# A two-layer Winograd convolution: fewer row operations in the input transform, two products added by TensorE onto used PSUM banks, 1/std inside VectorE's transform, fixed output buffers

## The chip, the cores and the metric

The kernel runs on one core of a Trainium2 chip. Five engines work side by side, each through its own list of instructions in order: TensorE (PE in the profile, its weight loads as PEld), VectorE (DVE), ScalarE (ACT), GpSimd (POOL), and SyncE (SP), which only issues DMAs here. They wait for each other by semaphores. The metric is the device time of the whole program in microseconds; shorter is better.

## The reference

Two equal layers, each a group normalisation (16 groups of 2 channels, no gain or bias), a 5x5 convolution with reflected edges, 32 to 32 channels, and a residual. The FFT in the reference is only one way to write the convolution.

```
def _gn(v, G=16, eps=1e-5):
    g = v.reshape(B_, G, C_ // G, H_, W_)
    m = jnp.mean(g, axis=(2, 3, 4), keepdims=True)
    s = jnp.var(g, axis=(2, 3, 4), keepdims=True)
    return ((g - m) / jnp.sqrt(s + eps)).reshape(v.shape)
...
xp = jnp.pad(x, ((0, 0), (0, 0), (2, 2), (2, 2)), mode='reflect')
...
# x: (8, 32, 252, 252) float32, weights (32, 32, 5, 5)
x = x + _L0_conv_ref(_gn(x), L0_conv_weight)
x = x + _L1_conv_ref(_gn(x), L1_conv_weight)
```

## The kernel before, in words

**Layout.** An image is split by the parity of its rows and columns into four planes; with 32 channels that makes 128 partitions. One parity row holds 126 values, padded to 128. In this layout the 5x5 filter is a 3x3 one with 128x128 matrices, and along the rows it is done as a Winograd transform F(6,3): 8 input rows become 8 transformed rows `v0`..`v7`, each takes part in one product (3 matmuls, one per column tap `b3`, 128x378, in float32, which the profile shows as two MATMUL records each, so 48 records a step), and the 8 products `m0`..`m7` are combined to 6 output rows.

**Steps.** A step (b, l, T) is 18 parity rows of image b in layer l (3 tiles of 6 rows). An image has 7 steps a layer (T = 0 to 6). The 112 steps stand in 16 phases of 7: (0,0), (1,0), (0,1), (2,0), (1,1), ... (7,0), (6,1), (7,1), written as (image, layer). The instruction order is written out by hand (`manual_schedule`); each engine runs its list in that order. What is written in iteration i of the main loop:

- SP: x of step i+4 (`fetch`, layer 0), two chunks of x for the statistics of a later image (`input_chunk`, three buffers `sx`), and the transformed weights `u` of the next phase at the phase's sixth step.
- DVE: `transform` of step i+1 (`e`, `p`, `q`, then `v1`..`v6`), then the output combination of step i.
- POOL: `differences` of step i+2 (`a` = rows 3-6 minus 1-4, `e` = rows 4-7 plus 0-3, over 4 rows each) and `ends` of step i+1 (`v0`, `v7` as two rows of differences of `e`). The first is held behind the last instruction of `transform` by a dependency of its own.
- PE: `m1`..`m6`, `m0`, `m7` of step i, each in a PSUM bank of its own (8 banks in turn).
- ACT: copies of `m1`, `m3`, `m5` out of PSUM (`a1`, `a3`, `a5`); after `a1` `prepare` of step i+3 (layer 0: four copies x to `g` and the padding columns; layer 1: DMAs from a scratch tensor instead); after `a3` and `a5` the outgoing work of step i-1 (layer 0: padding of y, DMAs to scratch, two passes for sums; layer 1: two pairs of copies into `o`, then DMAs to the output); after `a5` the sums of two chunks of x, in four steps of a phase.

`m1`'s copy adds the bias; DVE forms s1, d1 = a1 +- m2; then m3, m4 and m5, m6 are turned in place into difference and sum ("pairs"), and y takes `2^j` times the first pair and `0.5^j` times the second; at last `m0` is added to row 0 and `m7` to row 5.

**The boundary.** In the last step of a phase (`late`), the normalisation of the next phase is made: DVE takes mean and variance from a PSUM tile, ACT the square root, DVE 1/std with one Newton step (`scales`, six instructions on one value a partition), ACT multiplies the 128x3072 weights by it (`scale_matrices`), DVE adds the identity part for the residual (`add_own`). Before the change `scales` stands behind the whole transform, `scale_matrices` behind `a3`, and `add_own` behind the first pair.

An instruction that waits holds all behind it on its engine, so the order in these lists decides who waits for whom.

Of the kernel before, what the change touches and what calls it, by code (L numbers as in the profile page):

```python
# [48 lines left out]
P = 128  # L50
# [16 lines left out]
    (0.0, -2 / 9, -2 / 9, 4 / 90, 4 / 90, 8 / 45, 8 / 45, 1.0),  # L67
# [4 lines left out]
def tile_conv_preact_x2(ctx: ExitStack, tc: tile.TileContext, x: bass.AP, w0: bass.AP, w1: bass.AP, out: bass.AP):  # L72
# [12 lines left out]
    ypool = ctx.enter_context(tc.tile_pool(name="ypool", bufs=2))  # L85
# [3 lines left out]
    psum = ctx.enter_context(tc.tile_pool(name="psum", bufs=8, space=bass.MemoryType.PSUM))  # L89
# [84 lines left out]
    def transform_taps(t: bass.AP, r: bass.AP, s: bass.AP):  # L174
# [21 lines left out]
        v.tensor_copy(rf[7], t2)  # L196
# [110 lines left out]
    def scales(b: int, l: int):  # L307
# [7 lines left out]
        v.tensor_mul(fix, inv, inv)  # L315
        v.tensor_mul(fix, fix, var)  # L316
# [5 lines left out]
    ut, offset = {}, {}  # L322
# [6 lines left out]
    def add_own(b: int, l: int):  # L329
        u = ut[b, l]  # L330
        for pc, h in enumerate(halves):
            nc.vector.tensor_add(u[h, :, 1 + pc, h], u[h, :, 1 + pc, h], own[h])  # L332

    def find_offset(b: int, l: int):
        po = psum.tile([P, 1], F32, tag="m", name=f"po_{b}_{l}")
# [7 lines left out]
    last = {}  # L343

    def differences(v, b: int, l: int, T: int):

        g = gt[b, l, T]
        n = f"{b}_{l}_{T}"
        a = apool.tile([P, 4, NT, PB], F32, tag="a", name=f"a_{n}")
        e = apool.tile([P, 4, NT, PB], F32, tag="e", name=f"e_{n}")  # L350
        ins = v.tensor_sub(rows(a), rows(g[:, 3:7]), rows(g[:, 1:5]))  # L351
        at[b, l, T] = a, e
        return ins, lambda: v.tensor_add(rows(e), rows(g[:, 4:8]), rows(g[:, 0:4]))  # L353

    def transform(b: int, l: int, T: int):
        g = gt.pop((b, l, T))
        a, e = at[b, l, T]
# [3 lines left out]
        v07 = vpool.tile([P, 2, NT, PB], F32, tag="v07", name=f"v07_{n}")  # L361
# [3 lines left out]
        stt(rows(e), rows(g[:, 2:6]), -17 / 4, rows(e))  # L365
        stt(rows(p), rows(a[:, 0:2]), -1 / 4, rows(a[:, 2:4]))
        v.tensor_add(vs[0], e[:, 2], e[:, 1])
        v.tensor_sub(vs[1], e[:, 2], e[:, 1])
        yield
        stt(rows(q), rows(a[:, 0:2]), -4.0, rows(a[:, 2:4]))  # L370
# [3 lines left out]
        last["transform"] = stt(vs[5], q[:, 0], -0.5, q[:, 1])  # L374
        vt[b, l, T] = [v07[:, 0], *vs, v07[:, 1], v07]
        yield

    def ends(v, b: int, l: int, T: int):

        a, e = at.pop((b, l, T))  # L380
        v.tensor_sub(rows(vt[b, l, T].pop()), rows(e[:, 2:4]), rows(e[:, 0:2]))  # L381


    def conv(b: int, l: int, T: int, after_1, after_3, after_5):
        vs = vt.pop((b, l, T))
        n = f"{b}_{l}_{T}"
        u = ut[b, l]

        y = ypool.tile([P, GR * PB + 2], F32, tag="y", name=f"y_{n}")
# [3 lines left out]
        def product(f: int):  # L393
            ps = psum.tile([P, NT, NB], F32, tag="m", name=f"m{f}_{n}")
            for b3 in range(3):
                nc.tensor.matmul(  # L396
                    ps,
                    u[:, f, b3, :],
                    vs[f][:, :, 2 - b3 : 2 - b3 + NB],
                    start=(b3 == 0),  # L400
                    stop=(b3 == 2),
                )
            return ps
# [5 lines left out]
        stt = lambda o, i0, c, i1: v.scalar_tensor_tensor(o, i0, c, i1, ALU.mult, ALU.add)  # L409
        m1 = product(1)  # L410
# [3 lines left out]
        m2 = product(2)  # L414
# [3 lines left out]
        m3 = product(3)  # L418
# [3 lines left out]
        m4 = product(4)  # L422
# [5 lines left out]
        m5 = product(5)  # L428
# [3 lines left out]
        m6 = product(6)  # L432
# [5 lines left out]
        v.tensor_add(yo[0], m0, yo[0])  # L438
        m7 = product(7)
        v.tensor_add(yo[5], m7, yo[5])  # L440
        return y
# [60 lines left out]
    for k, (p, s0) in enumerate(begin.items()):  # L502
# [45 lines left out]
    differences(nc.vector, *steps[0])[1]()  # L548
# [17 lines left out]

    done = None
    for i, step in enumerate(steps):
        if i + 4 < N:
            fetch(*steps[i + 4])  # L570
        for b, c in chunk_load.get(i, []):
            chunks[b, c] = input_chunk(b, c)
        for p in mid.get(i, []):
            nc.sync.dma_start(ut[p], stored[p[1]])
        for p in late.get(i, []):
            variance(*p)
        for p in mid.get(i, []):
            collect(*p)
        if i + 1 < N:
            for _ in transform(*steps[i + 1]):  # L580
                pass
        if i + 2 < N:
            ins, rest = differences(nc.gpsimd, *steps[i + 2])
            tc.add_manual_dep(ins.ins, last["transform"].ins.name, beside, reason="one reader of two operands at a time")
        if i + 1 < N:
            ends(nc.gpsimd, *steps[i + 1])
        if i + 2 < N:
            rest()
        for p in late.get(i, []):
            scales(*p)  # L590

# [4 lines left out]
        def after_3():  # L596
            for p in late.get(i, []):
                scale_matrices(*p)
            if done:
                (b, l, T), y = done  # L600
# [6 lines left out]
        def after_5():  # L607
            if done:
                (b, l, T), y = done
# [4 lines left out]
            for b, c in chunk_sum.get(i, []):  # L614
                input_sums(b, c, chunks.pop((b, c)))
            for p in late.get(i, []):
                add_own(*p)
# [42 lines left out]
```

## Time and profile before

| what | value |
|---|---|
| time, median of 3 runs | 2009.51 us (2007.68 to 2011.52) |
| profiled execution, its own time | 2010.49 us |
| its span, first to last instruction | 2008.7 us |
| granted TensorE clock, mean | 0.956 |
| PE, DVE, ACT, POOL busy | 89%, 95%, 68%, 51% |
| steps that run free | 15.38 us each |

The profile is of one execution. "Busy" is the time in which an engine has an instruction; a DVE instruction that waits for a port counts as busy. Rows of the timeline give start, duration, engine, line, and what is written and read; in brackets stands idle time before the instruction and what ended it. Tables by stage give, for each stretch of time, the busy time of each engine, the granted clock, the busy share of the 16 DMA engines, and their rate. The mark of a step is here the start of DVE's instruction on line 424 (the first pair).

### The profile page before, as it was taken

What the parts mean: (1) busy time and instruction counts of PE and PEld (TensorE: products, weight loads), DVE (VectorE), ACT (ScalarE), POOL (GpSimd) and SP (SyncE); (2) the same over time, 40 slices, a digit from 0 to 9 for tenths busy, and PEclk for the clock granted to TensorE, in tenths of its full rate; (3) what the DMA queues carried; (4) which work ended last, traced back from release to release, by engine and by line L of the source; (5) the groups of instructions that cost most, each with busy time, mean ns of one, the idle gap of its engine ahead of it and who ended that gap; (6) DMA issues with size and microseconds to landing.
All of it is one profiled execution on the core that took longest, in us unless ns stands there. A gap on an engine that the chain in (4) does not pass through costs nothing.

```text
span 2008.7 us, 19828 instructions
## 1 busy us (share of the span) xinstructions
PE 1793.3 (89%) x5440; PEld 1045.9 (52%) x5440; DVE 1905.8 (95%) x3473; ACT 1373.6 (68%) x1649; POOL 1017.9 (51%) x410
## 2 busy tenths in 40 slices
PE   0689998989989898998989989898998989989897
PEld 0345554545545455554545545455554545545454
DVE  6698999999999999999999999999999999999997
ACT  5798855888368873787738886487955888344344
POOL 5654453555545455354645555455453545545452
PEclk9889998999989899998989989899998989989899
DMA  6977874987749776697767977499874987666453
GB/s 226 234 221 156 159 200 146 284 189 153 238 147 277 180 146 206 214 254 175 161 196 236 241 149 192 138 285 216 167 214 143 271 185 148 197 166 194 136 161 93
DMA packets 225664, 386.43 MB, mean 192 GB/s; under 512 B 25488, under 2 KB 200848, under 8 KB 212624
## 3 DMA queue, kind: packets, MB, share of 16 engines
q1 hardware_dynamic: 225552, 385.16, 72.8%
q8 instruction: 43, 0.70, 0.1%
q14 instruction: 69, 0.57, 0.1%
HBM read 249.77 MB, written 135.28 MB: 192 GB/s over the span
## 4 chain that ended last, share of the span: by engine, by line
DVE 39%; PE 33%; DMA 10%; ACT 9%; issue 4%; POOL 2%; SPq 2%; DVEq 0%; ACTq 0%; POOLq 0%
PE m L396 33%; DVE y L409 13%; DMA g<-scratch 7%; DVE v L364 4%; DVE e L364 3%; DVE mr L318 2%; DVE fix L316 2%; ACT g L151 2%; DMA x<-in_x_dram 2%; DVE p L364 2%; DVE q L364 2%; DVE m L424 1%; DVE fix L315 1%; DVE m L425 1%; ACT sx L276 1%
## 5 line engine op out<-in xcount | busy, mean ns | idle before, releaser
L396 PE MATMUL m<-v,u 128*128 128x378 f32 x5376 | 1785.0, 493 | 97.8 <-ACT u L327 32.3
L396 PEld LDWEIGHTS m<-v,u 128*128 128x128 f32 x5376 | 1034.2, 194 | 832.0 <-DVE u L332 34.8
L351 POOL TENSOR_TENSOR a<-g 128x1536 f32<-128x1536 f32 x111 | 384.2, 3461 | 941.9 <-DVE v L364 626.2
L353 POOL TENSOR_TENSOR e<-g 128x1536 f32<-128x1536 f32 x111 | 383.8, 3458 | 8.6
L409 DVE SCALAR_TENSOR_TENSOR y<-m,y 128x378 f32<-128x378 f32 x672 | 317.2, 539 | 0.5
L151 ACT COPY g<-x 64x2268 f32<-64x2268 f32 x112 | 257.7, 2301 | 41.3 <-DMA x<-in_x_dram 33.8
L481 ACT COPY o<-y 64x1134 f32<-64x1134 f32 x224 | 278.6, 1244 | 6.3 <-issue 3.3
L283 ACT ACTIVATE junk<-y 128x2268 bf16<-128x2268 f32 x112 | 234.7, 2095 | 1.4
L364 DVE SCALAR_TENSOR_TENSOR e<-g,e 128x1536 f32<-128x1536 f32 x112 | 195.8, 1748 | 14.1 <-POOL e L353 13.9
L381 POOL TENSOR_TENSOR v<-e 128x768 f32<-128x768 f32 x111 | 207.0, 1865 | 2.1 <-DVE e L364 2.1
L409 DVE SCALAR_TENSOR_TENSOR y<-m,d 128x378 f32<-128x378 f32 x336 | 181.3, 539 | 17.1 <-ACT o L481 17.1
L409 DVE SCALAR_TENSOR_TENSOR y<-m,s 128x378 f32<-128x378 f32 x336 | 181.2, 539 | 0.0
L412 ACT ACTIVATE a<-m,off 128x378 f32<-128x378 f32 x112 | 63.8, 570 | 151.1 <-PE m L396 150.9
L420 ACT COPY a<-m 128x378 f32<-128x378 f32 x112 | 53.3, 476 | 146.6 <-PE m L396 144.2
L277 ACT ACTIVATE sx<-sx 128x2016 f32<-128x2016 f32 x64 | 118.9, 1858 | 19.5 <-DVE sums L274 17.2
L327 ACT ACTIVATE u<-u,mr 128x3072 f32<-128x3072 f32 x15 | 42.8, 2856 | 128.0 <-DVE mr L318 128.0
L364 DVE SCALAR_TENSOR_TENSOR v<-q 128x384 f32<-128x384 f32 x224 | 114.9, 553 | 0.0
L364 DVE SCALAR_TENSOR_TENSOR v<-p 128x384 f32<-128x384 f32 x224 | 114.3, 550 | 0.0
L364 DVE SCALAR_TENSOR_TENSOR p<-a 128x768 f32<-128x768 f32 x112 | 107.0, 955 | 0.0
L364 DVE SCALAR_TENSOR_TENSOR q<-a 128x768 f32<-128x768 f32 x112 | 106.3, 949 | 0.0
L276 ACT ACTIVATE sx<-sx 128x2016 f32<-128x2016 f32 (+1 forms) x56 | 103.5, 1848 | 2.5 <-DMA sx<-in_x_dram 2.1
L152 ACT COPY g<-x 64x756 f32<-64x756 f32 x112 | 100.0, 893 | 0.0
(69 smaller groups left out, 1047.3 us busy)
## 6 DMA issues: line engine op xcount, KB each, us to landing
g<-scratch SPq DMA_DIRECT2D x56, 1152.0 KB, 7.7
out_dram<-o SPq DMA_DIRECT2D x672, 94.5 KB, 2.1
sx<-in_x_dram SPq DMA_DIRECT2D x56, 1008.0 KB, 4.9
x<-in_x_dram SPq DMA_DIRECT2D x88, 630.0 KB, 8.3
scratch<-y SPq DMA_DIRECT2D x112, 288.0 KB, 2.8
scratch<-y SPq DMA_DIRECT2D x112, 240.0 KB, 3.6
u<-raw SPq DMA_DIRECT2D x15, 1536.0 KB, 6.9
g<-scratch SPq DMA_DIRECT2D x56, 256.0 KB, 8.3
```

The lines of the kernel that those rows point to most:

```text
L151: nc.scalar.copy(to[:, 0:TR], t[:, 0:GR, cols].rearrange("p (t j) w -> p j t w", j=TR))
L152: nc.scalar.copy(to[:, TR:DR], t[:, 2:IR, cols].rearrange("p (t j) w -> p j t w", j=TR)[:, TR - 2 : TR])
L276: nc.scalar.activation(t, t, AF.Identity, accum_out=st[:, 0, c : c + 1])
L277: nc.scalar.activation(t, t, AF.Square, accum_out=st[:, 1, c : c + 1])
L283: nc.scalar.activation(junk, view, (AF.Identity, AF.Square)[k], accum_out=st[:, k, T : T + 1])
L351: ins = v.tensor_sub(rows(a), rows(g[:, 3:7]), rows(g[:, 1:5]))
L353: return ins, lambda: v.tensor_add(rows(e), rows(g[:, 4:8]), rows(g[:, 0:4]))
L364: stt = lambda o, i0, c, i1: v.scalar_tensor_tensor(o, i0, c, i1, ALU.mult, ALU.add)
L381: v.tensor_sub(rows(vt[b, l, T].pop()), rows(e[:, 2:4]), rows(e[:, 0:2]))
L396: nc.tensor.matmul(ps, u[:, f, b3, :], vs[f][:, :, 2 - b3 : 2 - b3 + NB], start=(b3 == 0), stop=(b3 == 2),)
L409: stt = lambda o, i0, c, i1: v.scalar_tensor_tensor(o, i0, c, i1, ALU.mult, ALU.add)
L481: nc.scalar.copy(o[halves[s], :, :, 1 - pc : W : 2].rearrange("p t j w -> p j t w"), yr[halves[pc], js, :, 1 : 1 + NB])
```

## The change

1. **Input transform.** `e` becomes two rows (1, 2 plus 5, 6) instead of four, so POOL's second operation and DVE's first one shrink from 1536 to 768 values a partition. `v0`, `v7` are now rows 6, 7 minus 0, 1 on POOL, plus -21/4 of `a` on DVE: one DVE operation of 768 more, while POOL's `ends` becomes the third operation of `differences`.
2. **m0 and m7 on the pairs' banks.** `m0` is accumulated by TensorE onto the bank in which DVE has left the sum of m5, m6; `m7`, with weights times 32, onto the bank with their difference. Rows 0 and 5 of y are then made by one operation each (`finish`), after the transform of the next iteration. DVE's second set of y operations goes from 6 to 4. `m1`, `m2` of the next step are issued ahead of `m0`, `m7` of this one (`first_products` in `following`). PSUM: 7 banks for products, one for the statistics.
3. **1/std.** `scales` stands in the middle of the transform with one instruction fewer (two TENSOR_TENSORs become one TENSOR_SCALAR), `scale_matrices` right behind it on ACT, ahead of `a1`; `add_own` at the end of the transform. POOL's `differences` waits for the last of these.
4. **y** lies in two fixed buffers instead of a pool of two. The chunk loads stand at the end of an iteration's DMAs.

```
-        ins = v.tensor_sub(rows(a), rows(g[:, 3:7]), rows(g[:, 1:5]))
-        return ins, lambda: v.tensor_add(rows(e), rows(g[:, 4:8]), rows(g[:, 0:4]))
+        first = v.tensor_sub(rows(a), rows(g[:, 3:7]), rows(g[:, 1:5]))
+        v.tensor_add(rows(e), rows(g[:, 5:7]), rows(g[:, 1:3]))
+        v.tensor_sub(rows(v07), rows(g[:, 6:8]), rows(g[:, 0:2]))
...
-        stt(rows(e), rows(g[:, 2:6]), -17 / 4, rows(e))
+        stt(rows(e), rows(g[:, 3:5]), -17 / 4, rows(e))
...
+        stt(rows(v07), rows(a[:, 1:3]), -21 / 4, rows(v07))
         stt(rows(q), rows(a[:, 0:2]), -4.0, rows(a[:, 2:4]))
...
-        v.tensor_mul(fix, inv, inv)
-        v.tensor_mul(fix, fix, var)
+        v.tensor_scalar(fix, inv, inv, var, ALU.mult, ALU.mult)
...
-        for j in (5, 0, 1, 2, 3, 4):
+        for j in range(1, 5):
             stt(yo[j], m5 if j % 2 else m6, 0.5**j, yo[j])
-        m0 = product(0)
-        v.tensor_add(yo[0], m0, yo[0])
-        m7 = product(7)
-        v.tensor_add(yo[5], m7, yo[5])
+        following()
+        product(b, l, vs, 0, n, m6)
+        product(b, l, vt.pop((b, l, T)), 7, n, m5)
+        def finish():
+            v.tensor_add(yo[0], m6, yo[0])
+            stt(yo[5], m5, 0.5**5, yo[5])
...
+        parts = transform(*steps[i + 1]) if i + 1 < N else iter(())
+        next(parts, None)
+        for p in late.get(i, []):
+            scales(*p)
+            scale_matrices(*p)
+        next(parts, None)
+        for p in late.get(i, []):
+            add_own(*p)
+        if done:
+            done[2]()
...
         def after_5():
             ...
             for b, c in chunk_sum.get(i, []):
                 input_sums(b, c, chunks.pop((b, c)))
+            for b, c in chunk_load.get(i, []):
+                chunks[b, c] = input_chunk(b, c)
```

How PE's list changes in a step: first before, steps (2,0,2) and (2,0,3); names are product, image, layer, step.

```order
L396 MATMUL m5_2_0_2_3090<-v5_2_0_2_2899,u0_89 128x378 x3
L396 MATMUL m6_2_0_2_3098<-v6_2_0_2_2900,u0_89 128x378 x3
L396 MATMUL m0_2_0_2_3110<-v07_2_0_2_2901,u0_89 128x378 x3
L396 MATMUL m7_2_0_2_3115<-v07_2_0_2_2901,u0_89 128x378 x3
L396 MATMUL m1_2_0_3_3144<-v1_2_0_3_3013,u0_89 128x378 x3
L396 MATMUL m2_2_0_3_3158<-v2_2_0_3_3014,u0_89 128x378 x3
L396 MATMUL m3_2_0_3_3166<-v3_2_0_3_3015,u0_89 128x378 x3
```

The same place of PE's list after the change.

```order
L387 MATMUL m5_2_0_2_2999<-v5_2_0_2_2818,u0_89 128x378 x3
L387 MATMUL m6_2_0_2_3007<-v6_2_0_2_2819,u0_89 128x378 x3
L387 MATMUL m1_2_0_3_3017<-v1_2_0_3_2928,u0_89 128x378 x3
L387 MATMUL m2_2_0_3_3021<-v2_2_0_3_2929,u0_89 128x378 x3
L387 MATMUL m6_2_0_2_3007<-v07_2_0_2_2729,u0_89 128x378 x3
L387 MATMUL m5_2_0_2_2999<-v07_2_0_2_2729,u0_89 128x378 x3
L387 MATMUL m3_2_0_3_3071<-v3_2_0_3_2930,u0_89 128x378 x3
```

`m1`, `m2` of the next step have moved ahead of the two products on `v07`, which now write the banks of `m6` and `m5`.

ACT's list in the last step before phase (2,0), before the change: `std` is the square root, `u0` the weights, `g` the input of a later step.

```order
L304 ACTIVATE std_2_0_2655<-var_2_0_2652 128x1
L412 ACTIVATE a1_0_1_6_2694<-m1_0_1_6_2690,off_0_1_1965 128x378
L151 COPY g_2_0_2_2696<-x_87 64x18x126
L152 COPY g_2_0_2_2696<-x_87 64x6x126
L151 COPY g_2_0_2_2696<-x_87 64x18x126
L152 COPY g_2_0_2_2696<-x_87 64x6x126
L134 COPY g_2_0_2_2696<-g_2_0_2_2696 64x24x2
L136 COPY g_2_0_2_2696<-g_2_0_2_2696 64x24 x2
L420 COPY a3_0_1_6_2716<-m3_0_1_6_2712 128x378
L327 ACTIVATE u0_89<-u0_89,mr_2_0_2682 128x3072
```

And after it.

```order
L307 ACTIVATE std_2_0_2583<-var_2_0_2580 128x1
L329 ACTIVATE u0_89<-u0_89,mr_2_0_2599 128x3072
L420 ACTIVATE a1_0_1_6_2622<-m1_0_1_6_2562,off_0_1_1903 128x378
L154 COPY g_2_0_2_2624<-x_87 64x18x126
L155 COPY g_2_0_2_2624<-x_87 64x6x126
L154 COPY g_2_0_2_2624<-x_87 64x18x126
L155 COPY g_2_0_2_2624<-x_87 64x6x126
L137 COPY g_2_0_2_2624<-g_2_0_2_2624 64x24x2
L139 COPY g_2_0_2_2624<-g_2_0_2_2624 64x24 x2
L427 COPY a3_0_1_6_2640<-m3_0_1_6_2636 128x378
```

The weights' scaling has moved from behind `a3` to ahead of `a1` and of the copies to `g`.

DVE's list in that kind of step, before phase (0,1) (the names have lost their last numbers), before the change.

```order
L364 SCALAR_TENSOR_TENSOR v_0_1_0_1853<-q_1_0_1856 128x384
L314 RECIPROCAL inv_1_1871<-std_1_1846 128x1
L315 TENSOR_TENSOR fix_1_1872<-inv_1_1871 128x1
L316 TENSOR_TENSOR fix_1_1872<-fix_1_1872,var_1_1843 128x1
L317 TENSOR_SCALAR fix_1_1872<-fix_1_1872 128x1
L318 TENSOR_TENSOR mr_1_1873<-inv_1_1871,fix_1_1872 128x1
L319 SCALAR_TENSOR_TENSOR mr_1_1873<-me_1_1841,mr_1_1873 128x1
L416 TENSOR_TENSOR s_1_0_6_1895<-m_1_0_6_1891,a_1_0_6_1885 128x378
```

DVE's list at the same point after the change.

```order
L372 TENSOR_TENSOR v_0_1_0_1802<-e_1_0_1714 128x384
L317 RECIPROCAL inv_1_1813<-std_1_1799 128x1
L318 TENSOR_SCALAR fix_1_1814<-inv_1_1813,var_1_1796 128x1
L319 TENSOR_SCALAR fix_1_1814<-fix_1_1814 128x1
L320 TENSOR_TENSOR mr_1_1815<-inv_1_1813,fix_1_1814 128x1
L321 SCALAR_TENSOR_TENSOR mr_1_1815<-me_1_1794,mr_1_1815 128x1
L368 SCALAR_TENSOR_TENSOR v_0_1_0_1715<-a_1_0_1713,v_0_1_0_1715 128x768
```

The six small operations have become five and moved from the transform's end, where POOL starts its `differences`, to its middle.

More of the change, by code (lines that the diff above doesn't have):

```diff
@@ L596, in after_3 @@
         def after_3():
-            for p in late.get(i, []):
-                scale_matrices(*p)
             if done:
-                (b, l, T), y = done
+                (b, l, T), y, _ = done
                 if l:
```

131 lines of the change are left out of this document (63 added, 68 removed).

## The prediction

> **What bounds the kernel now.** I read the page's head first, then the run by stages, then one free step and the boundary instruction by instruction.
>
> ```profile
> PE 1793.3 (89%) x5440; PEld 1045.9 (52%) x5440; DVE 1905.8 (95%) x3473; ACT 1373.6 (68%) x1649; POOL 1017.9 (51%) x410
> PEclk9889998999989899998989989899998989989899
> DVE 39%; PE 33%; DMA 10%; ACT 9%; issue 4%; POOL 2%; SPq 2%; DVEq 0%; ACTq 0%; POOLq 0%
> ```
>
> VectorE looks like the bound (95%), but the chain that ended last is split between VectorE and TensorE, and the granted clock dips regularly. The stages tell them apart; columns are the stretch, its length, busy time (instructions) of PE, PEld, DVE, ACT and POOL, clock, DMA share and GB/s:
>
> ```profile
> 83.30:180.10 96.80, 79.40 (x220) 44.82 (x221) 77.51 (x148) 94.95 (x118) 55.39 (x27) 0.89 0.81 214
> 1180.60:1242.10 61.50, 61.50 (x195) 36.67 (x194) 61.50 (x117) 47.94 (x64) 34.80 (x13) 1.00 0.73 160
> 1242.10:1299.40 57.30, 49.89 (x146) 28.30 (x145) 56.96 (x100) 20.87 (x33) 26.06 (x10) 0.91 0.59 186
> 1299.40:1366.80 67.40, 66.06 (x209) 39.09 (x208) 61.78 (x118) 59.62 (x66) 36.33 (x13) 1.00 0.83 255
> 1366.80:1422.00 55.20, 46.12 (x139) 26.59 (x138) 53.61 (x100) 43.98 (x47) 24.65 (x10) 0.94 0.85 188
> 1990.10:2008.70 18.60, 7.54 (x24) 4.16 (x22) 8.44 (x18) 8.69 (x8) 0.00 (x0) 0.84 0.53 125
> ```
>
> Row 1 is five steps of the first phase: ScalarE is busy 94.95 of 96.8 us, so it is the bound there. Row 2 is four free steps of a layer-0 phase, 15.38 us each, with VectorE and TensorE both full. Rows 3 and 5 are three steps each around a boundary, into a layer-1 and into a layer-0 phase; rows 4 and 6 are the four steps with chunk sums and the end.
>
> One free step of VectorE, start to start, and a long undisturbed stretch of TensorE:
>
> ```profile
> 1956.06 1.75 DVE L364 SCALAR_TENSOR_TENSOR e<-g,e 128x1536 f32<-128x1536 f32 x1
> 1957.73 0.95 DVE L364 SCALAR_TENSOR_TENSOR p<-a 128x768 f32<-128x768 f32 x1
> 1958.60 0.55 DVE L367 TENSOR_TENSOR v<-e 128x384 f32<-128x384 f32 x1
> ...
> 1960.40 1.02 DVE L364 SCALAR_TENSOR_TENSOR v<-p 128x384 f32<-128x384 f32 x2
> 1961.34 1.02 DVE L364 SCALAR_TENSOR_TENSOR v<-q 128x384 f32<-128x384 f32 x2
> 1962.28 0.54 DVE L416 TENSOR_TENSOR s<-m,a 128x378 f32<-128x378 f32 x1
> ...
> 1967.78 2.83 DVE L409 SCALAR_TENSOR_TENSOR y<-m,y 128x378 f32<-128x378 f32 x6
> 1970.53 0.54 DVE L438 TENSOR_TENSOR y<-m,y 128x378 f32<-128x378 f32 x1
> ...
> 1971.45 1.74 DVE L364 SCALAR_TENSOR_TENSOR e<-g,e 128x1536 f32<-128x1536 f32 x1
> 347.64 72.66 PE L396 MATMUL m<-v,u 128*128 128x378 f32 x228 [1.34 <-ACT a L412]
> ```
>
> VectorE starts an operation of 1536 values every 1.67 us, of 768 every 0.87, of 378 every 0.46 (six in 2.75). Its step is 1971.45 - 1956.06 = 15.39 us. TensorE's matmuls come every (72.66 - 0.48) / 227 = 0.318 us (0.48 being one matmul's shown length), so 48 of them take 15.24 us. A free step hangs on VectorE by only 0.15 us.
>
> **The change, part by part.**
>
> *VectorE's step.* The `e` operation falls from 1.67 to 0.87 (-0.80); the new operation on `v07` adds 0.87; two y operations go (-0.92). New step: 15.39 - 0.85 = 14.54 us. TensorE's stays at 15.24: the same 48 matmuls. That a matmul adds onto a bank VectorE has written is not in this trace; the nearest row is the second and third matmul of every product, which add onto a bank at the same 0.318 us, so I take no difference; no gain is possible, and I give no loss. The step becomes TensorE's, and saves 0.15 us instead of 0.85.
>
> *The new wait of TensorE* is that of `m0` for VectorE's last y operation on the pair, with `m7` and all of the next step's products behind it. From the start of `m0` (t = 0): `m0`, `m7` to 3.81, `m3`, `m4` to 7.62, `m5`, `m6` to 11.43, the next `m1`, `m2` to 15.24. VectorE, released about 0.27 us after `m6`'s slot (0.48 - 0.318, and an estimated 0.1 for the signal), needs a pair (0.92) and four y (1.84) and 0.1 to its end: 14.6. So the two products that were moved ahead cover the wait with 0.6 us to spare. VectorE then does transform (6.29), `finish` (0.92), s and d (0.92) until 22.6 = 15.24 + 7.4 and finds `m4` done at 7.9: it idles, TensorE does not. Price 0 where this holds; if nothing covered it, 3.2 us a step.
>
> *POOL* now does 3.46 + 1.87 + 1.87 = 7.2 us after the transform instead of 8.8.
>
> ```profile
> L351 POOL TENSOR_TENSOR a<-g 128x1536 f32<-128x1536 f32 x111 | 384.2, 3461 | 941.9 <-DVE v L364 626.2
> L381 POOL TENSOR_TENSOR v<-e 128x768 f32<-128x768 f32 x111 | 207.0, 1865 | 2.1 <-DVE e L364 2.1
> ```
>
> It has 15.24 - 6.29 = 8.95 us until the next transform: nothing on the path, with 1.7 us to spare.
>
> *The boundary.* Now:
>
> ```profile
> 49.07 0.16 DVE L315 TENSOR_TENSOR fix<-inv 128x1 f32<-128x1 f32 x1
> ...
> 310.68 3.42 DVE L315 TENSOR_TENSOR fix<-inv 128x1 f32<-128x1 f32 x1
> 314.13 1.73 DVE L316 TENSOR_TENSOR fix<-fix,var 128x1 f32<-128x1 f32 x1
> 316.09 3.27 DVE L318 TENSOR_TENSOR mr<-inv,fix 128x1 f32<-128x1 f32 x1
> 319.40 2.85 ACT L327 ACTIVATE u<-u,mr 128x3072 f32<-128x3072 f32 x1 [12.46 <-DVE mr L318]
> 324.07 1.40 DVE L332 TENSOR_TENSOR u<-u,own 64x512 f32<-64x512 f32 x2
> ```
>
> One value a partition takes 0.16 us while POOL is idle (at 49 us) and up to 3.42 while POOL runs. These three cost 8.4 us at this boundary. Moved ahead of POOL's start they cost 0.16 each, and the weights are ready before their first product. What is left on VectorE: mean and variance 0.5, `scales` 0.8, `add_own` 1.4, together 2.7 us. Its idle time in the loop above (0.5 before the first pair, 0.2 before the second, 0.6 before `m0`) takes 1.3; about 1.3 us stays as a stall of TensorE at 8 boundaries into layer 1.
>
> Into layer 0 (7 boundaries) ScalarE's new order counts: square root, weights, `a1`, seven copies to `g`, and only then `a3`.
>
> ```profile
> 429.59 0.56 ACT L412 ACTIVATE a<-m,off 128x378 f32<-128x378 f32 x1
> 430.05 2.30 ACT L151 COPY g<-x 64x2268 f32<-64x2268 f32 x1
> ...
> 436.94 0.48 ACT L420 COPY a<-m 128x378 f32<-128x378 f32 x1
> ```
>
> VectorE's transform begins at t = -0.9; 0.5 + 2.7 (half the transform) + 0.8 later, at 3.1, the weights' factor is there; weights to 6.0, `a1` to 6.6, copies 6.9 us, `a3` done at 14.0. VectorE, without this, would take `m3`, `m4` at 10.0. From 14.0: pair 0.92, y 2.75, pair 0.92, four y 1.84, so `m0` goes at 20.6 instead of 15.24: a stall of 5.4 us, of which the last 4.5 us without any matmul. Sum: 8 x 1.3 + 7 x 5.4 = 48 us.
>
> *The clock.* After each boundary it is halved for a while:
>
> ```profile
> 316.70:320.10 3.40, 0.35 (x2) 0.30 (x2) 3.37 (x4) 0.70 (x1) 2.65 (x1) 1.00 0.00 0
> 320.10:323.50 3.40, 1.20 (x2) 0.50 (x2) 3.40 (x8) 3.35 (x5) 0.00 (x0) 0.50 0.21 46
> 326.90:330.30 3.40, 3.40 (x7) 1.60 (x6) 3.40 (x9) 1.15 (x4) 0.00 (x0) 0.50 0.82 174
> 330.30:333.70 3.40, 3.40 (x12) 2.05 (x11) 3.40 (x6) 0.67 (x3) 0.00 (x0) 1.00 0.56 232
> ```
>
> A stretch of 3.4 us almost without matmuls is followed by 10.2 us at 0.50, and in the half-rate rows 7 matmuls pass instead of 12. Before, VectorE was behind anyway; in a TensorE-bound kernel such a stretch costs its half. The old stall lasts some 8 us (rows 1 and 2 and part of the next); of a 4.5 us stall I let half meet the condition, for 6.8 us at half rate: 7 x 0.5 x 3.4 = 12 us, between 0 and 7 x 5.1 = 36.
>
> The Trainium skill ("TensorE: Matmul & The Clock Gate", Part 1, "What's actually happening") says that the clock falls to half after an idle window of about 3.4 us and comes back after a busy one, the windows running freely; the trace agrees (0.50, in steps of 3.4 us). By that rule alone a 4.5 us stall holds a whole window one time in three, which would make this term about 8 us.
>
> *ScalarE with the chunk sums* (four steps in each of six phases): from `a5` to the end of the next `a1`.
>
> ```profile
> 353.66 0.47 ACT L430 COPY a<-m 128x378 f32<-128x378 f32 x1 [0.95 <-PE m L396]
> ...
> 364.43 0.56 ACT L412 ACTIVATE a<-m,off 128x378 f32<-128x378 f32 x1
> ```
>
> That is 11.3 us. With 7 banks, in some steps `m4` takes the bank that `a1` frees; then `m4`, `m5` (3.8) and a release (0.3) close a loop of 15.5 us. Price 24 x 0.26 = 6 us; what they lose now (row 4: 67.4 - 61.5 = 6 us a phase) goes, since SP's chunk loads, which wait for a sum, no longer stand ahead of the other DMAs.
>
> *The ends.* The first phase stays ScalarE's, whose work there is unchanged: its five steps end at about 178 us, 2 earlier by its idle time. At the end no other product covers the wait of `m0`, so behind the last pair come four y (1.9), 12 matmuls with their release (4.1) and `finish` (1.0), 7.0 us, in place of six y and two additions (2.75 + 1.0): 18.6 becomes 22 us.
>
> *Sum.* 178 + 106 steps x 15.24 (1615) + 48 + 12 + 6 + 22 = 1881 us of span. The profiled execution's own time was 1.8 above its span and 1.0 above the median of the runs, so 1882 there and about 1881 in the median; I say 1880.
>
> **The rivals.**
>
> 1. *DMA becomes the bound in the steps with chunk sums.* Row 4 moves 255 x 67.4 = 17.2 MB in four steps at a share of 0.83; in 4 x 15.5 us the share would be 0.90. If queues make these steps as long as now (16.85), 24 x 1.35 = 32 us more: 1912. For it: the share; against: a step's lead on every load. 0.13.
> 2. *Half clock after every boundary.* 15 x 3.4 = 51 instead of 12: 1920. For it: 15 of 15 do it now. Against: the stall is 1.3 us at 8 of them. 0.12. By the Trainium skill's rule above (same page and section) a 1.3 us stall holds no whole window.
> 3. *The cover of `m0` is short.* If VectorE arrives 0.5 us late each step, 106 x 0.5 = 53: 1933. The 0.6 us spare is small, the releases are modelled. 0.10.
> 4. *No ScalarE delay at layer-0 boundaries*, a1 running ahead somehow: 7 x 4.1 and the 12 us go: 1840. 0.07.
> 5. *Slower than before.* Copies to `g` stand between `a1` and `a3` in 56 steps. The waits for `a3` now:
>
> ```profile
> DVE m L424 <- ACT a L420: 25.8, 11, 5.4
> ```
>
> If `a1`, held by a `finish` that comes late, made each of the other 49 steps pay the 5.4 us seen at worst: 1880 + 265 = 2145; it decides from 2.7 us a step. In the loop `a1` is done at 14.2 and `a3` is wanted at 23: 1.4 us spare. 0.03.
>
> **How the numbers follow.** My own case has 0.55, with 1862 to 1900 from the clock term (0 to 36), 0.3 us of error at each stall, and 4 us at the ends. With rivals 1 and 2 it is 0.80: 1850 to 1925, the lower end taking in part of rival 4. A difference of under 0.2% (4 us) can't be told from none here. Faster by more: all but rival 5 and a sum of several misfortunes, 0.96; within: 0.01; slower: 0.03.
>
> **What would show it.** Right: PE at over 93% with free steps of 15.24 us and its pitch 0.318; VectorE idle before the first pair; `fix` and `mr` at 0.16; the first phase unchanged; waits of VectorE for `a3` in 7 boundary steps. Wrong: TensorE waiting for y on line 397 in free steps (rival 3), ScalarE or POOL waiting for DMA in the chunk steps (rival 1), the clock at 0.50 after layer-1 boundaries (rival 2), or the stretches at half rate longer than 7 us.

## The result, and the profile after

| | before | after |
|---|---|---|
| median of 4 runs | 2008.9 us (2007.7 to 2011.5) | 1928.9 us (1927.7 to 1930.6) |
| span of the profiled execution | 2008.7 us | 1926.6 us |
| granted clock, mean | 0.956 | 0.971 |

The ratio is 0.960 (95% interval 0.958 to 0.962). 1880 was predicted, with 1850 to 1925: 49 us too little, and 4 us outside the range.

From the head of the page after:

```profile
PE 1762.5 (91%) x5440; PEld 1041.3 (54%) x5440; DVE 1729.5 (90%) x3345; ACT 1377.4 (71%) x1649; POOL 827.9 (43%) x410
PEclk9789999999999999998999999999999999999999
PE 55%; DVE 18%; ACT 12%; DMA 8%; issue 4%; POOL 2%; SPq 2%; ACTq 0%; DVEq 0%; POOLq 0%
```

TensorE is the bound now, but only 55% of the chain is its own; ScalarE still holds 12%. The stages (columns as in the prediction): five steps of the first phase; four free steps; into layer 1 (two steps); three steps with chunk sums; the fourth of these with the next step; into layer 0 (two steps); the end.

```profile
84.20:189.80 105.60, 81.20 (x217) 46.44 (x218) 75.17 (x142) 93.71 (x121) 46.87 (x25) 0.85 0.78 194
471.60:532.60 61.00, 61.00 (x193) 36.29 (x192) 58.97 (x114) 39.17 (x55) 28.07 (x13) 1.00 0.71 181
532.60:564.70 32.10, 31.16 (x101) 18.51 (x100) 31.80 (x66) 15.08 (x24) 13.56 (x7) 1.00 0.73 218
564.70:610.40 45.70, 45.70 (x145) 27.22 (x144) 44.20 (x85) 42.77 (x47) 21.60 (x10) 1.00 0.91 296
610.40:646.90 36.50, 32.45 (x97) 18.84 (x96) 29.43 (x57) 33.52 (x37) 15.11 (x7) 0.95 0.90 199
646.90:685.10 38.20, 33.46 (x101) 19.63 (x100) 31.99 (x66) 29.34 (x32) 14.71 (x8) 0.91 0.77 177
1904.80:1926.60 21.80, 9.48 (x24) 4.88 (x22) 7.71 (x16) 8.66 (x8) 0.00 (x0) 0.81 0.45 107
```

Rows 2 and 4 are TensorE without a hole: 15.24 us a step. Row 3 is 1.6 us over two free steps. Rows 1, 5 and 6 hold the loss: row 1 took 96.8 us before, row 5 is 6.0 and row 6 is 7.7 us over two free steps (30.5). Laid beside the terms of the sum:

| term | predicted | measured |
|---|---|---|
| first phase, to the mark of its step 5 | 178 | 189.8 |
| 106 steps of 15.24 | 1615 | 1615 |
| 8 boundaries into layer 1 | 10 | 8 x 1.65 = 13 |
| 7 into layer 0, half clock included | 38 + 12 = 50 | 7 x 7.5 = 53 |
| chunk sums, 6 phases | 6 | 6 x 5.7 = 34 |
| end | 22 | 21.8 |
| span | 1881 | 1927 |

Two terms failed: the first phase (+12) and the chunk sums (+28). The fourth row hides two errors that cancel (see below).

**The first phase.** VectorE, POOL and ScalarE in the step that lost most, from the timeline after:

```profile
94.66 3.44 POOL L354 TENSOR_TENSOR a<-g 128x1536 f32<-128x1536 f32 x1
98.06 1.80 POOL L355 TENSOR_TENSOR e<-g 128x768 f32<-128x768 f32 x1
...
99.90 2.55 DVE L368 SCALAR_TENSOR_TENSOR e<-g,e 128x768 f32<-128x768 f32 x1 [9.20 <-POOL e L355]
...
108.25 0.53 DVE L397 SCALAR_TENSOR_TENSOR y<-m,y 128x378 f32<-128x378 f32 x1
...
108.82 0.26 ACT L137 COPY y<-y 64x36 f32<-64x36 f32 x1 [9.09 <-DVE y L397]
```

POOL has the second layer's filter to transform and begins `differences` of step 2 only at 94.66. VectorE's transform waits for it until 99.90, and `finish` of step 0 stands behind that transform in VectorE's list. So y is complete at 108.8, and ScalarE, the bound in this phase, stands idle for 9.1 us.

**The last chunk sums.** ScalarE, VectorE and TensorE in the steps T = 3 and 4 of phase (1,1):

```profile
610.44 0.56 DVE L431 TENSOR_TENSOR m<-a,m 128x378 f32<-128x378 f32 x1 [0.47 <-PE m L387]
...
612.27 0.47 ACT L437 COPY a<-m 128x378 f32<-128x378 f32 x1 [0.92 <-PE m L387]
...
615.29 1.88 ACT L279 ACTIVATE sx<-sx 128x2016 f32<-128x2016 f32 x1
...
622.64 0.56 ACT L420 ACTIVATE a<-m,off 128x378 f32<-128x378 f32 x1
623.22 2.31 ACT L154 COPY g<-x 64x2268 f32<-64x2268 f32 x1
...
630.17 0.47 ACT L427 COPY a<-m 128x378 f32<-128x378 f32 x1
...
630.67 0.56 DVE L431 TENSOR_TENSOR m<-a,m 128x378 f32<-128x378 f32 x1 [5.46 <-ACT a L427]
...
637.24 13.39 PE L387 MATMUL m<-v,u 128*128 128x378 f32 x36 [4.04 <-DVE y L397]
```

Behind `a5` come the output copies, the sums of two chunks (615.29 to 622.6), `a1`, and then the first copies to `g` for the next layer-0 phase (623.22 to 630.1); only then `a3`. VectorE waits 5.46 us for it, TensorE 4.04 us for VectorE's y, and a window at half clock follows. This is the queue that the prediction worked out for the late step, two steps earlier.

### The profile page after: what moved, and what is told of

It reads as the page before. It is cut to its first block, busy times and chain, and to the rows that moved or that the text cites. A ratio compares the mean times of both kernels' runs of the same rounds, so it can differ in the third digit from the quotient of the medians.

```text
span 1926.6 us, 19376 instructions
## 1 busy us (share of the span) xinstructions
PE 1762.5 (91%) x5440; PEld 1041.3 (54%) x5440; DVE 1729.5 (90%) x3345; ACT 1377.4 (71%) x1649; POOL 827.9 (43%) x410
## 4 chain that ended last, share of the span: by engine, by line
PE 55%; DVE 18%; ACT 12%; DMA 8%; issue 4%; POOL 2%; SPq 2%; ACTq 0%; DVEq 0%; POOLq 0%
PE m L387 55%; DVE y L397 8%; ACT g L154 4%; DMA x<-in_x_dram 3%; DMA out_dram<-o 1%; ACT g L155 1%; DMA g<-scratch 1%; DVE v L368 1%; ACT sx L279 1%; ACT o L492 1%; ACT sx L280 1%; DMA sx<-in_x_dram 1%; DVE m L440 1%; DVE m L432 1%; DVE m L441 1%
## 5 line engine op out<-in xcount | busy, mean ns | idle before, releaser
L387 PE MATMUL m<-v,u 128*128 128x378 f32 x5376 | 1761.3, 489 | 105.2 <-DVE y L397 88.7
L397 DVE SCALAR_TENSOR_TENSOR y<-m,y 128x378 f32<-128x378 f32 x560 | 275.5, 542 | 2.9 <-PE m L387 2.9
L356 POOL TENSOR_TENSOR v<-g 128x768 f32<-128x768 f32 x111 | 202.6, 1825 | 0.0
L355 POOL TENSOR_TENSOR e<-g 128x768 f32<-128x768 f32 x111 | 202.6, 1825 | 0.0
L431 DVE TENSOR_TENSOR m<-a,m 128x378 f32<-128x378 f32 x112 | 62.2, 556 | 125.0 <-ACT a L427 69.9
L280 ACT ACTIVATE sx<-sx 128x2016 f32<-128x2016 f32 x64 | 118.9, 1857 | 19.7 <-DVE sums L277 17.4
L368 DVE SCALAR_TENSOR_TENSOR e<-g,e 128x768 f32<-128x768 f32 x112 | 108.5, 969 | 9.2 <-POOL e L355 9.2
L368 DVE SCALAR_TENSOR_TENSOR v<-a,v 128x768 f32<-128x768 f32 x112 | 106.6, 952 | 0.0
```

The costliest lines, as they stand in the source:

```text
L280: nc.scalar.activation(t, t, AF.Square, accum_out=st[:, 1, c : c + 1])
L355: v.tensor_add(rows(e), rows(g[:, 5:7]), rows(g[:, 1:3]))
L356: v.tensor_sub(rows(v07), rows(g[:, 6:8]), rows(g[:, 0:2]))
L387: nc.tensor.matmul(ps, ut[b, l][:, f, b3, :], vs[f][:, :, 2 - b3 : 2 - b3 + NB], start=(b3 == 0 and onto is None), stop=(b3 == 2), skip_gr ...
L397: stt = lambda o, i0, c, i1: nc.vector.scalar_tensor_tensor(o, i0, c, i1, ALU.mult, ALU.add)
```

## The experiments

Times are medians; before took 2008 to 2011 us beside them.

| kernel | us | ratio to before (95%) |
|---|---|---|
| after | 1928.9 | 0.960 (0.958 to 0.962) |
| e1 copies to `g` behind `a5` | 1890.0 | 0.941 (0.938 to 0.943) |
| e2 without the last sums | 1896.7 | 0.944 (0.942 to 0.946) |
| e3 `finish` first in step 1 | 1922.4 | 0.957 (0.955 to 0.959) |
| e4 no cover of `m0` | 2548.3 | 1.268 (1.265 to 1.272) |
| e5 e1 and e3 | 1882.1 | 0.936 (0.933 to 0.938) |
| e6 before + place of 1/std | 1931.8 | 0.961 (0.959 to 0.963) |
| e7 after, 1/std in its old place | 1960.2 | 0.975 (0.973 to 0.977) |
| e8 after, chunk loads in their old place | 1992.9 | 0.991 (0.989 to 0.993) |
| e9 e3, sums earlier, copies behind `a5` in some steps | 1905.0 | 0.948 (0.947 to 0.950) |
| e10 e6 + chunk loads behind | 1908.9 | 0.950 (0.949 to 0.951) |
| e11 e4 and e1 | 2397.4 | 1.193 (1.191 to 1.196) |
| e12 before's arithmetic, order of e9 | 1881.2 | 0.937 (0.935 to 0.938) |
| e13 e9 with the sums elsewhere | 1850.1 | 0.921 (0.919 to 0.922) |
| e14 before, `scales` with one tensor input each | 1959.4 | 0.975 (0.974 to 0.977) |
| e15 before's arithmetic, order of e13 | 1877.5 | 0.935 (0.933 to 0.936) |

**Where the two terms went (e3, e2, e1, e5).**

e3 moves one call, in step 1 alone:

```
+        early = done and i == 1
+        if early:
+            done[2]()
         parts = transform(*steps[i + 1]) if i + 1 < N else iter(())
...
-        if done:
+        if done and not early:
             done[2]()
```

> Theory: the first phase lost 9.1 us because the last two y operations of step 0 stood behind a transform that waited for POOL, and ScalarE, the bound there, waited for y. With finish ahead of the transform in step 1 alone, that wait goes: mark of step 5 at about 181 instead of 190, 1920 us. Rival (ScalarE is held by loads of x or of chunks there, and the wait only changes its name): under 3 us, 1926 to 1930.

The first phase by its stage:

```profile
84.20:181.00 96.80, 76.54 (x220) 44.17 (x221) 74.93 (x142) 93.74 (x119) 46.68 (x25) 0.91 0.84 211
```

Five steps take 96.8 us as before, with the same work of ScalarE (93.7). The mark is at 181.0 as expected, and the median falls by 6.5 us (9 expected).

e2 leaves the last sums out:

```
             for b, c in chunk_sum.get(i, []):
-                input_sums(b, c, chunks.pop((b, c)))
+                t = chunks.pop((b, c))
+                if b == 1 or c < 6:
+                    input_sums(b, c, t)
```

> Leaves out ScalarE's sums of chunks 6 and 7 of images 2 to 7 (the statistics use six chunks). Theory: the loss at T = 3 to 5 of a layer-1 phase comes from these last sums (7.4 us) and the copies to g right behind them, so it goes: 6 x 5.9 = 35 us, 1894 us, and the boundaries into layer 0 stay as they are. Rival (the copies alone, or their loads, make that loss): the steps stay at 20.1 and 16.2 us, 1929 us.

It won 32 us. Step T = 3 falls from 20.1 to 15.24 us in three of the six phases and to between 15.8 and 16.9 in the others, T = 4 from 16.2 to between 15.1 and 16.0; the step before a boundary (T = 5) stays at 21. In the worst of these T = 3 steps ScalarE waits for a load of x ahead of the copies:

```profile
1060.05 2.29 ACT L154 COPY g<-x 64x2268 f32<-64x2268 f32 x1 [3.28 <-DMA x<-in_x_dram]
```

e1 moves the copies:

```
         def after_1():
-            if i + 3 < N:
-                prepare(*steps[i + 3])
+            pass
...
         def after_5():
+            if i + 3 < N:
+                prepare(*steps[i + 3])
             if done:
```

> Theory: where ScalarE comes late (at the last chunk sums, and behind the weights' factor into layer 0), the 6.9 us of copies to g stand ahead of a3 and VectorE and TensorE wait for them. With the copies behind a5, the 5.9 us in each of 6 layer-1 phases go (35 us) and the 7.7 us at 7 boundaries into layer 0 fall to the 1.6 us of the others (43 us): 1929 - 78 = 1851 us. Rival (the stalls are VectorE's added work or the half clock by itself): less than 10 us are won, about 1925.

39 us won, half of what was expected. Step T = 3 is at 15.24 and the wait for `a3` is gone, but the six phases take 113.3 us in the mean, not 108.3, and a step of the first phase rose from 17.2 to 23.2. The queue on ScalarE is as long as it was, and what stands behind the copies is late instead: in the first phase the chunk sums, for which VectorE waits ahead of its transform (8.49 us, 2.25 after the change), and at the boundary the square root:

```profile
187.56 0.17 DVE L290 TENSOR_REDUCE tot<-sums 128x2 f32<-128x16 f32 x1 [8.49 <-ACT sx L280]
...
426.04 0.20 ACT L307 ACTIVATE std<-var 128x1 f32<-128x1 f32 x1
426.27 0.17 DVE L317 RECIPROCAL inv<-std 128x1 f32<-128x1 f32 x1 [1.51 <-ACT std L307]
```

The square root now stands behind copies and output, and VectorE waits 1.51 us for it in the middle of its transform.

e5 is e1 with e3.

> Copies to g behind a5, and finish ahead of the transform in step 1. If both theories hold and do not touch each other: 1929 - 78 - 9 = 1842 us. If the stalls are VectorE's own work and the first phase hangs on loads: about 1925.

8 us under e1 (the step that lost most takes 18.8 us instead of 25.8), so e3's gain comes on top; e1's shortfall stays, and the step of 23.2 us with it.

**The order that mends both (e9, e13).** e9 is e3 with two more moves: the sums and their loads stand four steps earlier, and the copies stand behind `a5` in the layer-0 phases after the first and in the last step of each phase, elsewhere in their old place:

```
-                at_step = s0 - 7 + c // 2 if k > 1 else c * 5 // 8
+                at_step = s0 - 11 + c // 2 if k > 1 else c * 5 // 8
...
+        behind = i >= NG and (step[1] == 0 or step[2] == NG - 1)
         def after_1():
-            if i + 3 < N:
+            if i + 3 < N and not behind:
                 prepare(*steps[i + 3])
         def after_5():
+            if i + 3 < N and behind:
+                prepare(*steps[i + 3])
```

> Three moves: finish ahead of the transform in step 1; the chunk sums and loads four steps earlier (T = 3 to 6 of the layer-0 phase before, where ScalarE is busy 6.4 us of 15.24); the copies to g behind a5 in layer-0 phases and at T = 6. Theory: the six layer-1 phases in front of a layer-0 phase fall from 120.1 to about 109.5 us, the first phase by 8: 1929 - 64 - 7 = 1858 us. Rival (chunk loads collide with the stores to scratch and the loads of g in the layer-0 phases): their steps T = 3 to 6 rise over 15.24 us, and no more than 1880 is reached.

The layer-1 phases are at 108.3 us, but the six layer-0 phases that now hold the sums rose to 117.4, so the rival's number (over 1880) came true. The rival named the loads; the timeline shows ScalarE's queue, with no wait for a load in it. At T = 3 the sums meet the copies and VectorE waits 5.71 us for `a1`; at T = 5 the square root stands behind the sums, until 539.10, and VectorE waits 2.57 us for it:

```profile
511.42 0.55 DVE L423 TENSOR_TENSOR s<-m,a 128x378 f32<-128x378 f32 x1 [5.71 <-ACT a L420]
...
537.22 1.88 ACT L280 ACTIVATE sx<-sx 128x2016 f32<-128x2016 f32 x1
...
539.10 0.19 ACT L307 ACTIVATE std<-var 128x1 f32<-128x1 f32 x1
539.32 0.17 DVE L317 RECIPROCAL inv<-std 128x1 f32<-128x1 f32 x1 [2.57 <-ACT std L307]
```

e13 puts the sums where neither is near:

```
+                at_step = (s0 - 10, s0 - 7, s0 - 6, s0 - 5)[c // 2] if k > 1 else c * 5 // 8
```

> As e9, with the chunk sums at T = 4 of the layer-0 phase and T = 0, 1, 2 of the layer-1 phase, so that neither the copies to g, nor the square root and the weights' factor at a boundary stand behind them. Theory (the rest of e9's loss is that its sums met the copies at T = 3, and at T = 5 the square root of a boundary): every phase takes 108.3 us: 84 + 135 + 14 x 108.3 + 113 = 1848 us of span. Rival (chunk loads beside the stores to scratch): the layer-0 phases stay over 112 us and the time over 1875.

Its page, and six steps of which two form a boundary into layer 1:

```profile
PE 1735.8 (94%) x5440; PEld 1029.3 (56%) x5440; DVE 1729.5 (94%) x3345; ACT 1380.9 (75%) x1649; POOL 829.0 (45%) x410
PEclk9889999999999999999999999999999999999999
449.50:510.50 61.00, 61.00 (x194) 36.33 (x193) 58.94 (x114) 53.50 (x70) 28.12 (x13) 1.00 0.78 211
525.50:557.70 32.20, 31.25 (x100) 18.48 (x99) 32.11 (x63) 20.86 (x32) 14.96 (x7) 1.00 0.79 251
```

The span is 1848.2 us, as worked out, and all 14 phases between the first and the last take 108.3 to 108.4 us. The boundaries into layer 0 cost the same 1.6 us as the others. e13 does the same arithmetic as after, is 79 us faster, and beats both kernels.

**What each part is worth (e6, e7, e14, e10, e8, e12, e15).**

e6 is before with `scales`, `scale_matrices` and `add_own` moved into the transform:

> The kernel before with the place of 1/std and the weights' factor alone changed. Theory (the gain lies at the boundaries): 8 boundaries into layer 1 lose their 8.5 us of waits and 7 into layer 0 some 3.7 us, since there ScalarE's copies come next: 2009 - 94 = about 1915, no slower than the whole change. Rival (the shorter VectorE step and the additions on TensorE carry the gain): less than 40 us, over 1970.

e6 is 79 us under the runs of before beside it (2011.0): by itself as much as the whole change (80). The phases that end in a boundary into layer 1 fell from 118.9 to 111.0 us (8 as expected). At the boundaries into layer 0 nothing was won (3.7 expected): the steps T = 5 and 6 took 38.4 us together before and take 39.1 to 39.3 here, since VectorE now waits for `a3` behind the copies to `g`, as the prediction had it for the changed kernel:

```profile
436.22 0.56 DVE L424 TENSOR_TENSOR m<-a,m 128x378 f32<-128x378 f32 x1 [5.16 <-ACT a L420]
```

These phases are about 2 us shorter all the same, by their steps with chunk sums; why was not followed up.

e7 is the counterpart: the changed kernel with these three back where they were.

> The changed kernel with 1/std and the weights' factor back in their old place. Theory (the gain lies at the boundaries): the waits of 8.4 us and the half clock return, some 12 us at 8 boundaries and 4 us at 7: about 2050, as slow as before or slower. Rival (the other parts carry the gain): under 1960.

Only 31 us lost, a quarter of the forecast: 4.8 us at each boundary into layer 1, while those into layer 0 are 1 us shorter than after the change. VectorE and POOL there:

```profile
318.60 0.27 DVE L318 TENSOR_SCALAR fix<-inv,var 128x1 f32<-128x1 f32 x1
...
319.10 2.06 DVE L320 TENSOR_TENSOR mr<-inv,fix 128x1 f32<-128x1 f32 x1
321.20 1.74 DVE L321 SCALAR_TENSOR_TENSOR mr<-me,mr 128x1 f32<-128x1 f32 x1
...
317.71 3.44 POOL L354 TENSOR_TENSOR a<-g 128x1536 f32<-128x1536 f32 x1 [8.65 <-issue]
```

`mr` ends at 319.10 + 2.06 = 321.16, with POOL's operation (317.71 + 3.44 = 321.15). `fix`, now one TENSOR_SCALAR, runs in the middle of it and takes 0.27 us. So it may be the operations with two tensor inputs that wait, and the fused `fix` may have taken about half of the wait already (2.06 + 1.74 us are left of 8.4). e14 tries that on the kernel before, with the place of `scales` unchanged:

```
-        v.tensor_mul(fix, inv, inv)
-        v.tensor_mul(fix, fix, var)
+        v.tensor_scalar(fix, inv, inv, var, ALU.mult, ALU.mult)
...
-        v.tensor_mul(mr[:, 0:1], inv, fix)
-        v.scalar_tensor_tensor(mr[:, 1:2], me[:, 0:1], -1.0, mr[:, 0:1], ALU.mult, ALU.mult)
+        v.tensor_scalar(mr[:, 0:1], inv, fix, None, ALU.mult)
+        v.tensor_scalar(mr[:, 1:2], me[:, 0:1], mr[:, 0:1], -1.0, ALU.mult, ALU.mult)
```

> The kernel before with the four operations of scales that have two or more tensors of one value a partition written as tensor_scalar, the other values as scalar operands; their place stays behind POOL's start. Theory (an operation with two tensor inputs in SBUF waits until POOL's running operation ends, one with one tensor input does not): they take 0.3 us at most each, 7 to 8 us go at each boundary into layer 1 and some 2 into layer 0: 2008 - 75 = about 1933 us. Rival (any small operation waits while POOL runs): 2.0 to 3.4 us each as before, 2008 us.

```profile
309.96 3.46 POOL L350 TENSOR_TENSOR a<-g 128x1536 f32<-128x1536 f32 x1 [7.12 <-DVE inv L314]
...
309.99 0.27 DVE L315 TENSOR_SCALAR fix<-inv,var 128x1 f32<-128x1 f32 x1
...
310.74 0.21 DVE L318 TENSOR_SCALAR mr<-me,mr 128x1 f32<-128x1 f32 x1
...
315.45 4.54 DVE L331 TENSOR_TENSOR u<-u,own 64x512 f32<-64x512 f32 x2
```

The four have become three, and all three run beside POOL's `a` (the middle one, L317, too) in 0.21 to 0.27 us: shown. 49 us went instead of 75. The step T = 5 before a boundary into layer 1 fell from 24.9 to 17.0 us, but T = 6 rose from 16.95 to 20.1: the next operation with two tensors in SBUF, `add_own`, now meets POOL and takes 4.54 us for the pair instead of 1.40.

e8 puts the chunk loads back at the head of the iteration.

> The changed kernel with the chunk loads issued at the head of the step again, as before. Theory of the prediction: they wait for a sum ahead of SP's other loads, 6 us in each of 6 layer-1 phases: 1965 us. Rival (that loss before had another cause): 1929 us.

64 us lost, 10.8 in the mean of the six phases. Waits of SP's and VectorE's lists between 340 and 415 us of it:

```profile
SPq L271 <- ACT sx L280: 29.8, 3, 17.2
DVE y L397 <- DMA scratch<-y: 5.4, 1, 5.4
```

SP holds a chunk load until a sum has freed its buffer, 17.2 us at the longest, and the stores of y to scratch stand behind it; VectorE then waits for a y buffer.

e10 gives the kernel before both moves, 1/std and the loads behind the sums.

> The kernel before with two parts alone: 1/std inside the transform, and the chunk loads issued behind the sums. Theory: the 4.7 us by which the steps with chunk sums still exceed 15.38 go in 6 phases: 1932 - 28 = 1904 us, faster than the whole change; then the input transform, the additions on TensorE and the fixed y buffers cost 25 us as they stand. Rival: the loads are hidden in VectorE's order, 1932 us.

It took 1908.9 us: two moves of order, without the new arithmetic, beat the whole change by 20 us. Why the chunk sums did not hurt there is seen in the same step T = 3 to 4:

```profile
370.99 0.47 ACT L430 COPY a<-m 128x378 f32<-128x378 f32 x1 [0.93 <-PE m L396]
...
374.47 0.56 DVE L424 TENSOR_TENSOR m<-a,m 128x378 f32<-128x378 f32 x1
...
388.77 0.47 ACT L420 COPY a<-m 128x378 f32<-128x378 f32 x1
...
389.85 0.57 DVE L424 TENSOR_TENSOR m<-a,m 128x378 f32<-128x378 f32 x1
```

In the old order TensorE runs ahead of VectorE, and `a5` is copied 3.5 us before VectorE's mark; after the change it is copied 1.8 us behind it (612.27 against 610.44). ScalarE does the same queue in 17.8 to 17.9 us (370.99 to 388.77, 612.27 to 630.17): then it was 0.6 us early, now it is 5.5 late. The new arithmetic took 5.3 us of lead from ScalarE. The reason is argued, not shown by a run: `m5` now stands behind an `m0` that can't start before VectorE's pair of the step before, and VectorE's own step is shorter than TensorE's.

e12 and e15 give the old arithmetic the order of e9 and of e13 as well.

> The arithmetic of the kernel before (six-row transform, y additions on VectorE) with the order of e9: 1/std inside the transform, loads behind the sums, sums four steps earlier, copies behind a5. Theory: VectorE's step of 15.38 us and its 2.7 us at each boundary: 83 + 136 + 14 phases of about 110.6 + 105 = 1873 us, so that the new arithmetic, unhindered, is worth about 15 us. Rival (the new arithmetic is worth nothing at all): equal to e9 within 4 us; or it carries more: over 1890.

> The arithmetic of the kernel before in the order of e13 (copies to g behind a5 in layer-0 phases and at T = 6, sums at T = 4 of the layer-0 phase and T = 0, 1, 2). Theory: the 5 us that e12 lost at its one T = 3 of phase (1,0) go, nothing else: 1876 us, so that the input transform, the additions on TensorE and the fixed buffers are worth 26 us where nothing else is in their way, of which 106 x 0.15 = 16 us come from the free steps. Rival (they gain by the order alone): within 5 us of e13, 1850.

e12 took 1881.2, with 20.4 us in one step T = 3 that e15 does not have: in the order of e9 the new arithmetic (1905.0) costs 24 us, where the theory gave it a gain of 15. e15 took 1877.5. Against it e13 is 27 us faster: 14 phases of 108.3 us instead of 110.9 give 36, and the last phase takes 8 back (112.8 against 104.6), since there TensorE ran ahead in the old order. Of the 2.6 us a phase, 7 x 0.15 = 1 come from the free steps and the rest from the boundary. There VectorE is the bound in both kernels (busy 32.11 of 32.20 us in e13's last row above, 33.61 of 33.90 us at such a place in e15), so that its shorter step counts in full. The new arithmetic is thus worth 27 us where ScalarE is in nobody's way, and as it stood it cost 20.

**The cover of `m0` (e4, e11).** e4 puts `following()` behind `m0` and `m7`.

> The next step's m1 and m2 go behind m0 and m7 again. Theory (cover): TensorE then waits in each step for a pair and four y operations, 3.2 us: about 105 x 3.2 = 336 us more, 2265 us. Rival (VectorE is early enough without the cover): under 5 us, about 1930.

The sign was right, the size not: 619 us were lost. One step of a layer-1 phase takes 20.2 us, another 18.5. Windows of 3.41 us at two of these stalls of 3.0 us:

```profile
431.90:435.31 3.41, 1.21 (x4) 0.83 (x5) 3.41 (x7) 3.35 (x4) 0.00 (x0) 1.00 0.62 143
435.31:438.72 3.41, 3.41 (x7) 1.72 (x6) 3.41 (x6) 3.38 (x5) 0.00 (x0) 0.50 0.94 281
452.38:455.79 3.41, 1.49 (x5) 0.97 (x6) 3.41 (x7) 3.35 (x4) 0.00 (x0) 1.00 0.63 148
455.79:459.20 3.41, 3.41 (x13) 2.00 (x12) 3.41 (x7) 3.38 (x5) 0.00 (x0) 1.00 0.96 288
```

A window with 1.21 us of matmuls is followed by one at half clock (7 matmuls instead of 13), one with 1.49 us is not. So the step is 15.24 + 3.27, and 1.7 us more where the stall lies badly. In layer-0 steps of e4 there is a second wait, of VectorE for `a3` behind the copies to `g`:

```profile
276.12 0.56 DVE L431 TENSOR_TENSOR m<-a,m 128x378 f32<-128x378 f32 x1 [4.95 <-ACT a L427]
```

e11 takes that one away by e1's edit.

> m1 and m2 behind m0 and m7 again, and the copies to g behind a5. Theory: without the cover, a1 comes late, and in layer-0 steps the copies behind it made VectorE wait another 5 us for a3; with them out of the way every free step takes 18.5 us at full clock, or 20.2 with one 3.4 us window at half clock: 2548 - 150 = about 2390 us. Rival (the half clock alone made the steps of layer 0 longer): over 2500 us.

2397.4 us: 151 went, and the free steps of all phases are at 20.2, a few at 18.5.

## Why the prediction was right and wrong

- **Free step, pitch, cover: right.** The new matmuls onto banks that VectorE wrote come at (67.47 - 0.48) / 211 = 0.3175 us:

```profile
463.74 67.47 PE L387 MATMUL m<-v,u 128*128 128x378 f32 x212
```

  Free steps are 15.24 us, TensorE waits in none of them, and e4 shows the 3.2 us that the cover hides (3.27 a step at full clock; rival 3 false).
- **Boundaries: right in kind; in size, into layer 0, partly by luck.** 1.65 us into layer 1 (1.3 predicted), and 7.5 into layer 0, the half clock included (5.4 + 1.7). The parts were each off: in the sixth stage row TensorE is without matmuls for 38.2 - 33.5 = 4.7 us, not 5.4, and the clock is at half for 6.8 us (0.91 of full in the mean), which costs some 3 us, not 1.7. `scales` takes 0.15 to 0.27 us an operation, clear of POOL:

```profile
656.87 0.27 DVE L318 TENSOR_SCALAR fix<-inv,var 128x1 f32<-128x1 f32 x1
...
657.36 0.16 DVE L320 TENSOR_TENSOR mr<-inv,fix 128x1 f32<-128x1 f32 x1
```

  The wait for `a3` there was ScalarE's queue as predicted: where it was mended (e13) 6 us a boundary went. Rivals 2 and 4 are false: no half clock follows a boundary into layer 1 (third stage row, clock 1.00), and the delay into layer 0 was there.
- **"ScalarE with the chunk sums ... 24 x 0.26 = 6 us": the step that failed most.** It asked for `a1` alone. The first three steps cost nothing; the fourth, where the copies to `g` set in behind the same sums, cost 5.7 us a phase, 34 in all. The prediction had the queue of copies ahead of `a3` in its boundary term, and did not ask where else ScalarE enters it late. Its own figures held the loss: `m5`'s slot ends at 9.5, so `a5` starts at 9.8; `a1` ends 11.3 later, at 21.1; 6.9 of copies and 0.5 for `a3` make 28.5, where VectorE wants it at 23. That is 5.5 us late, and 5.46 were measured. (The loop of 15.5 us in that term adds up to 15.4, and `m0`'s start of 20.6 in the boundary term to 20.5; neither matters.)
- **"The first phase stays ScalarE's ... at about 178": failed.** ScalarE's work is the same, but its release is not: `finish` stands behind a transform that waits for POOL (e3: 9 us at the mark). Of the other 3 us, 2 are a gain that was predicted and that e3 does not show either, and 0.9 lies ahead of the first mark (84.2 us, 83.3 before).
- **DMA (rival 1): false.** The share rose to 0.91 in the steps with sums (fourth stage row, 296 GB/s), and they stayed at 15.24.
- **The loads behind the sums: right in kind; the size depends on the rest of the order.** 6 us a phase were claimed; e8 shows 10.8 in the changed kernel, and e10 against e6 shows 23 us or 3.8 a phase with the old arithmetic.
- **Rival 5 did not come, but half of its mechanism is real:** a late `a1` with the copies ahead of `a3` is the loss at the last sums, where the sums make `a1` late, and in e4's layer-0 steps it comes nearly every time.

Open: the input transform, the additions on TensorE, the fixed y buffers and the seven banks in place of eight were only tried together, so what each of them is worth is not shown.

## What to carry to other kernels

When an edit ties an engine to another within each step (here TensorE to VectorE's last y), the engines behind lose the lead that they had: work out each queue's slack again, at every place where two loads meet on it, the prologue included, not only at the one that the edit touches. Try the parts of a change alone, and the new order without the new arithmetic: here two moves of order gave more than the whole, and the arithmetic paid only after ScalarE's list had been mended.

## What the hardware showed beside

- **The half clock needs no empty window.** The record of the clock goes in windows of 3.41 us. Over the 17 kernels here, each window at full clock whose matmuls filled 0.40 of it or less was followed by one at half clock, and none that was filled to more than 0.45; between these both occur. Full clock came back after each half-rate window that was filled to 0.87 or more, and after none with 0.82 or less (busy shares by the profile, whose matmul ends are modelled). The Trainium skill ("TensorE: Matmul & The Clock Gate", Part 1, "HAM oscillation — how this bites in real kernels") gives as the rule that gaps must stay under some 3.4 us; here stalls of 3.0 us brought the half clock in most free steps of e4's layer-1 phases (20.2 us 23 times, 18.5 four times), so the measurement decides. After the change it is seen behind the stall of 4.04 us, where matmuls filled 1.26 of 3.40 us (0.37).

- **Which small operations wait for POOL is a matter of their form.** One value a partition took 1.7 to 3.4 us with two tensors in SBUF, until POOL's operation ended (before, e7), and 0.21 to 0.27 us with one tensor and scalar operands (e14). VectorE's additions with one operand in PSUM ran at 0.54 us beside POOL. The Trainium skill ("SBUF — State Buffer", "Who interferes with whom") states this for two inputs against a POOL operation that reads; the traces agree, and show that scalar operands read from SBUF do not count as the second one.
